# A two-layer graph network on one core: means of x taken on ScalarE and sent through DRAM, and sums and folds moved to other places

## The chip, the cores and the metric

The kernel runs on one NeuronCore of a Trainium2 chip. The metric is device time in microseconds for one launch that computes the whole output. The kernel before was run nine times; the median is 2200.85 us (2199.92 to 2202.66).

The engines are named as in the profile: PE is TensorE (matmuls; PEld its weight loads), DVE is VectorE, ACT is ScalarE, POOL is GpSimd, and SP issues most DMAs. A trailing q (SPq, PEq) means the engine's instruction queue.

## What is computed

There are 16 batches of x, 1024 nodes by 256 channels, and one adjacency matrix of 1024 by 1024. The reference, cut to what matters:

```python
# layer 0: attention whose queries come from a weighted adjacency
fea = transpose(x)                                # B, C, N
c = mean(fea, axis=1)                             # mean of x over channels: B, N
A = abs(abs(sigmoid(c[:, None, :] - c[:, :, None]) - 0.5) - 0.5) * 2
g = relu(einsum('bcn,bnm->bcm', fea, adj * A) * para)
q = heads(transpose(g));  k, v = heads(x @ kv_w)
out = softmax(q @ k.T * scale) @ v                # 4 heads of 64
x = layernorm(x + out)
# layer 1: two graph convolutions
h = relu(x @ w1_loop + adj @ (x @ w1_neigh) + b1)
h = relu(h @ w2_loop + adj @ (h @ w2_neigh) + b2)
x = layernorm(x + (x + h) * 0.5)
```

All data is float32. The channel means c enter as a row over all partitions (`c_row`) and as a column of one value per node (`c_col`); the weights of a node tile are the tanh of a scaled |c_col − c_row|, plus one, times adj.

## The kernel before

**Batches overlap.** The loop over b runs the attention of batch b in four units (two pairs of heads by two halves of the nodes). A unit's scores are eight pairs of matmuls (`s`, L516), each followed by an exponential on ACT (`pr`, L519); DVE adds the exponentials up (`acc`, L523 and L525), transposes the sum (`accB`, L527) and reduces it (`den_part`, L529). Then 32 matmuls (L536) weigh the values into `av`, which DVE transposes into `o` (L540). The softmax's denominators are finished in `add(u)`: a small matmul with the matrix `fold` (L548) sums over the 32-row groups, and DVE divides, adds to the residual `xB_a` and reduces `sums`.

In the gaps between the units stand the convolutions of earlier batches (c1, c2 and c3 are batches b−1, b−2 and b−3) and the preparation of batch b+1: `gap0` after unit 0, `gap1` after unit 1, `gap2` after unit 2. From batch 2 on, two convolutions run together as `both`, a seven-product scheme (`Joined.run`, products in the order 1, 2, 6, 7, 5, 4, 3), whose argument names the functions to be called after each product. Batch 1 has only one convolution and takes the `else` branch of gap1, with `c1.first`. Batches 2 to 14 are called the fast batches here; they all run the same instructions.

**Means before.** `prepare` (L244) transposes the channel-blocked load of x into `xT` and reduces it over the 32 channels of each block (`part`, L249, two reduces and a `join`). `means` (L262) folds `part` over partitions with one small matmul (`mean_ps`, L256), scales it, transposes a broadcast of it into `c_row` (L267), and picks `c_col` out of it with the matrix `quarter` (L269 and L272). In a fast batch it is called after product 2, in batch 1 at the head of gap1, in batch 0 between steps 6 and 7 of the queries.

**Queries.** `FastQueries` forms g with a seven-product scheme too: `step(k)` for k = 0 to 3 accumulates seven products in PSUM, two in each of three large tiles (a, b, c) and one in a bank; `end` copies product 1 to SBUF (`P1`, L482), combines them with seven adds on DVE (L483 to L489), multiplies by para (L491) and applies relu on ACT (L492). Batches 0 and 1 use the plain `Queries` (L400, end at L406 and L407).

**Normalisation.** `BlockedNorm.mean` subtracts the mean (L312). `squares` squares on ACT (L318) and reduces on DVE (L319, `sq_part`, and a join). `variance` folds that with a small matmul (`sum_ps`, L256), scales (L324) and takes the power −0.5 on POOL (L326). `scale` multiplies (L331), and `spread` transposes to `x1T` (L216) and stores to DRAM (`x1d`, L339), from which the next convolutions read.

**Keys and values.** `keys` runs two groups of eight matmuls (`k_ps`, L350), with the function `between` (the variance) called ahead of the second, and copies each group to `kT` on ACT (L352). `values` runs four groups of eight (`v_ps`, L362), each in a one-bank PSUM tile, of which there are two (`bank`, bufs=2), copied on ACT (L364). Large PSUM tiles (`big`) are three.

**Order.** The whole of `run` is under a manual schedule: each engine and each DMA queue executes in the order in which the source calls it. SBUF tiles of 128x1024 come from one pool of 23 (`row`); a tile waits until an earlier user of its buffer is through.

**Start.** x of batch 0 comes in four quarters (L117); 16 transposes on PE (L227) make its xT, then keys and values follow. `tiles` are column-blocked loads of adj (`adj_blocked`, L207) which `turn_adj` transposes on DVE (L871), in batch 1; `adj_sums` forms four sums of those tables and stores them.

Of the kernel before, what the change touches and what calls it, by code (L numbers as in the profile page):

```python
# [10 lines left out]
F32 = mybir.dt.float32  # L11
I32 = mybir.dt.int32
AF = mybir.ActivationFunctionType
# [5 lines left out]
def kernel(  # L19
# [136 lines left out]
    quarter = const.tile([P, Q], F32, name="quarter")  # L156
    nc.vector.tensor_reduce(quarter, ident.rearrange("p (i k) -> p i k", k=S), AX.X, ALU.add)
# [86 lines left out]
    def prepare(blocked, name):  # L244

        xT = channel_major(blocked, f"xT_{name}")
        part = small.tile([P, NC, NB], F32, tag="part", name=f"part_{name}", bufs=2)
        for cc in range(NC):
            nc.vector.tensor_reduce(part[:, cc, :], blocked[cc].rearrange("p (bn r) -> p bn r", r=S), AX.X, ALU.add)  # L249
        join(part)  # L250
        return xT, part

# [9 lines left out]
    def means(part, name):  # L262

        mean = small.tile([P, NB], F32, tag="mean", name=f"mean_{name}", bufs=2)
        nc.vector.tensor_scalar_mul(mean, fold_sums(part, f"mean_{name}"), 1.0 / C)
        c_row = work.tile([P, N], F32, tag="c_row", name=f"c_row_{name}")
        nc.vector.transpose(c_row.rearrange("p (bn k) -> p bn k", k=S), mean.unsqueeze(2).to_broadcast([P, NB, S]))  # L267
        own = small.tile([P, NT, Q], F32, tag="own", name=f"own_{name}", bufs=1)
        nc.vector.tensor_mul(own, mean.rearrange("p (t i) -> p t i", i=Q),  # L269
                             quarter.unsqueeze(1).to_broadcast([P, NT, Q]))  # L270
        c_col = small.tile([P, NT], F32, tag="c_col", name=f"c_col_{name}", bufs=2)
        nc.vector.tensor_reduce(c_col, own, AX.X, ALU.add)  # L272
        return c_row, c_col
# [27 lines left out]
    class BlockedNorm:  # L301
# [12 lines left out]
        def squares(self):  # L314
            self.part = small.tile([P, NC, NB], F32, tag="part", name=f"sq_part_{self.name}", bufs=2)
            for cc in range(NC):
                sq = row_tile(f"sq_{self.name}_{cc}")
                nc.scalar.activation(sq, self.xB[cc], AF.Square)  # L318
                nc.vector.tensor_reduce(self.part[:, cc, :], by_node(sq), AX.X, ALU.add)  # L319
            join(self.part)  # L320
# [89 lines left out]
    class FastQueries(Queries):  # L410
# [64 lines left out]
        def end(self):  # L475
# [10 lines left out]
            add(qT[:, 1, h0], u[:, h1], p[4])  # L486
            add(qT[:, 1, h1], u[:, h1], p[5])
# [131 lines left out]
    class GraphConv:  # L619
# [214 lines left out]
    def run():  # L834
# [5 lines left out]

        xT, c_col = prepare_first(x_first)
# [4 lines left out]
        blocked = load_blocked(1, "1")  # L846
        load_weights()
# [12 lines left out]
        tiles = {}  # L860
# [12 lines left out]
        for t in range(NT):  # L873
# [3 lines left out]
            if t == 4:  # L877
                xB = load_blocked(0, "a0")
                ready = {}
                ready["xT"], ready["part"] = prepare(blocked, "1")  # L880
            if t == 6:
                ready["mean"] = means(ready["part"], "1")
        qT = q.end()
        convs = {}
        for b in range(B):
# [9 lines left out]
            def gap0():  # L895
                blocked = load_blocked(b + 1, str(b + 1))
                c1.inner()
# [5 lines left out]
                ready["xT"], ready["part"] = prepare(blocked, str(b + 1))  # L903
# [5 lines left out]

            def next_means():  # L910
# [203 lines left out]
```

## Time and profile before

| What | Value |
|---|---|
| median of 9 runs | 2200.85 us |
| profiled execution | 2200.99 us |
| its span, first to last instruction | 2199.1 us |
| mean granted TensorE clock | 0.997 of full speed |
| first scores of batches 0, 1, 2 | 51.77, 151.50, 277.09 us |
| from one fast batch to the next | 134.7 to 135.3 us |
| DMA: x of the next batch, issue to landing | 7.2 us median |

The time that counts is the device time of a run; the profile's span leaves out some 2 us around the first and the last instruction. In the timeline a row gives the start in microseconds from the span's start, the length, engine, line, operation, tile written <- tiles read, shape, and the number of instructions merged; in brackets stands how long the engine idled before and what ended it. In the list of waits a row gives who waited for whom, the sum in microseconds, the number of times, and the longest. A matmul's length counts its way through the array; the next starts earlier. The chain that ended last (its first line gives 63% to PE, 29% to DVE) is read with care, since it names DVE's adds wherever an exponential's consumer was a bit later.

### The profile page before, as it was taken

What the parts mean: (1) busy time and instruction counts of PE and PEld (TensorE: products, weight loads), DVE (VectorE), ACT (ScalarE), POOL (GpSimd) and SP (SyncE); (2) the same over time, 40 slices, a digit from 0 to 9 for tenths busy, and PEclk for the clock granted to TensorE, in tenths of its full rate; (3) what the DMA queues carried; (4) which work ended last, traced back from release to release, by engine and by line L of the source; (5) the groups of instructions that cost most, each with busy time, mean ns of one, the idle gap of its engine ahead of it and who ended that gap; (6) DMA issues with size and microseconds to landing.
All of it is one profiled execution on the core that took longest, in us unless ns stands there. A gap on an engine that the chain in (4) does not pass through costs nothing.

```text
span 2199.1 us, 22720 instructions
## 1 busy us (share of the span) xinstructions
PE 2172.6 (99%) x8096; PEld 1031.7 (47%) x8096; DVE 1865.5 (85%) x2453; ACT 969.4 (44%) x1064; POOL 328.6 (15%) x177
## 2 busy tenths in 40 slices
PE   8998999999999999999999999999999999999998
PEld 4344444544444444444444445444454444544354
DVE  4988888898898988988889788998989889888965
ACT  4734445434354443545444454534544445434511
POOL 1010020210302103021030301203012020210021
PEclk9999999999999999999999999999999999999999
DMA  8294262633646335463453735526354262633342
GB/s 193 87 139 148 58 182 68 123 126 65 175 101 148 106 59 175 93 172 92 73 161 77 182 87 79 171 58 182 86 94 156 58 182 87 130 120 65 116 134 97
DMA packets 586359, 258.59 MB, mean 118 GB/s; under 512 B 488064, under 2 KB 552448, under 8 KB 586240
## 3 DMA queue, kind: packets, MB, share of 16 engines
q1 hardware_dynamic: 585968, 256.56, 47.9%
q8 instruction: 65, 1.06, 0.2%
q14 instruction: 54, 0.44, 0.1%
q10 hardware_dynamic: 272, 0.52, 0.1%
HBM read 210.90 MB, written 46.14 MB: 117 GB/s over the span
## 4 chain that ended last, share of the span: by engine, by line
PE 63%; DVE 29%; SPq 3%; issue 2%; DMA 1%; ACT 1%; POOL 1%; DVEq 0%; ACTq 0%
PE hu_ps L793 15%; PE s L516 13%; PE av L536 12%; DVE acc L525 7%; PE k_ps L350 4%; PE v_ps L362 4%; PE h_ps L700 2%; PE g_ps L400 2%; PE h_ps L701 2%; DVE wg L392 2%; PE hu_ps L641 2%; SPq L108 2%; PE t_ps L634 2%; DVE sq_part L319 1%; DVE wg L446 1%
## 5 line engine op out<-in xcount | busy, mean ns | idle before, releaser
L519 ACT ACTIVATE pr<-s 128x1024 f32<-128x1024 f32 x512 | 476.2, 1052 | 179.4 <-PE s L516 179.1
L525 DVE TENSOR_TENSOR acc<-acc,pr 128x1024 f32<-128x1024 f32 x384 | 493.2, 1284 | 41.4 <-DVE acc L525 0.9
L516 PE MATMUL s<-qT,kT 64*128 64x512 f32 x2048 | 457.2, 596 | 0.7 <-ACT qT L407 0.7
L536 PE MATMUL av<-pr,v 128*64 128x512 f32 x2048 | 453.6, 595 | 0.0
L516 PEld LDWEIGHTS s<-qT,kT 64*128 64x128 f32 x2048 | 190.9, 186 | 236.5 <-ACT pr L519 114.8
L536 PEld LDWEIGHTS av<-pr,v 128*64 128x64 f32 x2048 | 141.3, 137 | 300.1 <-issue 289.8
L326 POOL TENSOR_TENSOR rstd<-rstd,neg_half 128x32 f32<-128x32 f32 x16 | 87.1, 5441 | 1148.0 <-DVE rstd L324 1148.0
L386 ACT ACTIVATE wg<-c_row,c_col 128x1024 f32<-128x1024 f32 x128 | 147.1, 1149 | 87.1 <-DVE accB L527 50.6
L793 PE MATMUL hu_ps<-adj,R 128*128 128x512 f32 x360 | 158.3, 596 | 0.0
L392 DVE SCALAR_TENSOR_TENSOR wg<-wg,adj 128x1024 f32<-128x1024 f32 x128 | 149.8, 1210 | 9.8 <-ACT wg L387 9.8
L387 ACT ACTIVATE wg<-wg 128x1024 f32<-128x1024 f32 x128 | 135.4, 1058 | 4.1
L350 PE MATMUL k_ps<-xT,kvw_sb 128*128 128x512 f32 x256 | 117.2, 602 | 2.8 <-DVE U L483 2.5
L318 ACT ACTIVATE sq<-xB_a 128x1024 f32<-128x1024 f32 x32 | 33.8, 1057 | 192.3 <-DVE xB_a L312 178.7
L473 PE MATMUL g_ps<-wg,S 128*128 128x512 f32 x224 | 116.7, 603 | 0.0
L473 PE MATMUL g_ps<-T,S 128*128 128x512 f32 x224 | 114.4, 592 | 0.0
L362 PE MATMUL v_ps<-kvw_sb,xT 128*128 128x256 f32 x512 | 113.1, 379 | 0.0
L331 DVE TENSOR_TENSOR xB_a<-xB_a,rstd 128x1024 f32<-128x1024 f32 x32 | 38.8, 1254 | 84.4 <-POOL rstd L326 84.4
L473 PE MATMUL g_ps<-wg,x 128*128 128x512 f32 x224 | 109.0, 599 | 0.0
L362 PEld LDWEIGHTS v_ps<-kvw_sb,xT 128*128 128x128 f32 x512 | 97.3, 190 | 20.1 <-issue 7.7
L523 DVE TENSOR_TENSOR acc<-pr,pr 128x1024 f32<-128x1024 f32 x64 | 78.0, 1219 | 33.6 <-ACT pr L519 33.6
L793 PE MATMUL hu_ps<-adjT,t 128*128 128x512 f32 x240 | 105.7, 592 | 0.0
L793 PEld LDWEIGHTS hu_ps<-adj,R 128*128 128x128 f32 x360 | 67.3, 190 | 78.9 <-issue 74.6
(167 smaller groups left out, 2719.5 us busy)
## 6 DMA issues: line engine op xcount, KB each, us to landing
adj<-in_adj_dram SPq DMA_DIRECT2D x128, 512.0 KB, 4.5
adj<-adjT SPq DMA_DIRECT2D x120, 512.0 KB, 7.8
xB_a<-in_x_dram SPq DMA_DIRECT2D x128, 128.0 KB, 4.1
x1d<-xB_a SPq DMA_DIRECT2D x128, 128.0 KB, 3.4
x<-x1d SPq DMA_DIRECT2D x16, 1024.0 KB, 6.7
xB<-in_x_dram SPq DMA_DIRECT2D x120, 128.0 KB, 4.7
x<-in_x_dram SPq DMA_DIRECT2D x15, 1024.0 KB, 7.2
out_dram<-x SPq DMA_DIRECT2D x15, 1024.0 KB, 4.6
```

What stands on the lines that cost most here:

```text
L326: nc.gpsimd.tensor_tensor(self.rstd, self.rstd, neg_half, ALU.pow)
L350: nc.tensor.matmul(pk[:, ts(j, FB)], kvw_sb[:, cc, ts(kb, P)], xT[:, cc, ts(j, FB)], start=(cc == 0), stop=(cc == NC - 1))
L362: nc.tensor.matmul(pv[:, ts(i, C)], xT[:, cc, ts(g * per + i, P)], kvw_sb[:, cc, C:2 * C], start=(cc == 0), stop=(cc == NC - 1))
L386: nc.scalar.activation(wg, self.c_row, AF.Abs, bias=self.c_col[:, t:t + 1], scale=-1.0)
L387: nc.scalar.activation(wg, wg, AF.Tanh, scale=-0.5)
L392: nc.vector.scalar_tensor_tensor(wg, wg, 1.0, self.adj.pop(t), op0=ALU.add, op1=ALU.mult)
L473: nc.tensor.matmul(self.p[n], x_n[:, k, :], w_n, start=(k == 0), stop=(k == TJ - 1))
L516: nc.tensor.matmul(ps[:, ts(s, FB)], self.kT[rows, pair, ts(mt, P)], self.qT[rows, pair, ts(j, FB)], start=True, stop=True)
L519: nc.scalar.activation(pr, ps, AF.Exp)
L525: nc.vector.tensor_add(acc, acc, pr)
L536: nc.tensor.matmul(pav[s * HD:(s + 1) * HD, :], self.v[:, mt, pair * P + s * HD:pair * P + (s + 1) * HD], self.pr[mt][:, ts(s, FB)], start ...
L793: nc.tensor.matmul(dst, self.x[n][:, k, :], half_adj[w][:, k, :] if w else of_rows(rows, k), start=(start and k == 0), stop=(k == TJ - 1), ...
```

## The change

- The means are no longer reduced on DVE. ACT runs eight `Identity` instructions over x (128x256 each, written back in place), whose accumulator gives the node sums; POOL scales them to `c_col`. SP writes `c_col` to a line in DRAM and reads it back broadcast over 128 partitions as `c_row`. `quarter`, `prepare` and the fold of the means on PE go.
- `means` is called in gap0, right after the issue of the next batch's blocked load; for batch 0 after unit 0.
- The row sums of the squares (`sum_squares`) are split from `squares` and called inside `end`, after four of the seven adds. In the plain batch and the last batch they follow `squares` as before.
- The seven products of the queries are spread over the PSUM tiles in another way: tile b holds products 2 and 7, tile c 5 and 3.
- `keys` calls `between` later: after half of the second group.
- In batch 1, `add(1)`, `adj_sums` and the first weighing move into `c1.first`, after four of its eight node tiles.
- Before x arrives, PE runs 16 transposes of the identity into a tile that nobody reads.
- Three of the eight table loads `adj_blocked` move to the start, ahead of the weights, and their turns from batch 1 to batch 0 (step 4 of the queries).

```diff
-    quarter = const.tile([P, Q], F32, name="quarter")
-    nc.vector.tensor_reduce(quarter, ident.rearrange("p (i k) -> p i k", k=S), AX.X, ALU.add)
...
-    def prepare(blocked, name):
-
-        xT = channel_major(blocked, f"xT_{name}")
-        part = small.tile([P, NC, NB], F32, tag="part", name=f"part_{name}", bufs=2)
-        for cc in range(NC):
-            nc.vector.tensor_reduce(part[:, cc, :], blocked[cc].rearrange("p (bn r) -> p bn r", r=S), AX.X, ALU.add)
-        join(part)
-        return xT, part
...
-    def means(part, name):
-
-        mean = small.tile([P, NB], F32, tag="mean", name=f"mean_{name}", bufs=2)
-        nc.vector.tensor_scalar_mul(mean, fold_sums(part, f"mean_{name}"), 1.0 / C)
+    def means(xb, name):
+
+        c_col = small.tile([P, NT], F32, tag="c_col", name=f"c_col_{name}", bufs=2)
+        for t in range(NT):
+            nc.scalar.activation(xb[:, t, :], xb[:, t, :], AF.Identity, accum_out=c_col[:, t:t + 1])
+        nc.gpsimd.tensor_scalar_mul(c_col, c_col, 1.0 / C)
+        line = dram.tile([1, N], F32, tag="line", name=f"line_{name}")
+        nc.sync.dma_start(out=line.rearrange("o (t p) -> p (o t)", p=P), in_=c_col)
         c_row = work.tile([P, N], F32, tag="c_row", name=f"c_row_{name}")
-        nc.vector.transpose(c_row.rearrange("p (bn k) -> p bn k", k=S), mean.unsqueeze(2).to_broadcast([P, NB, S]))
-        own = small.tile([P, NT, Q], F32, tag="own", name=f"own_{name}", bufs=1)
-        nc.vector.tensor_mul(own, mean.rearrange("p (t i) -> p t i", i=Q),
-                             quarter.unsqueeze(1).to_broadcast([P, NT, Q]))
-        c_col = small.tile([P, NT], F32, tag="c_col", name=f"c_col_{name}", bufs=2)
-        nc.vector.tensor_reduce(c_col, own, AX.X, ALU.add)
+        nc.sync.dma_start(out=c_row, in_=line.to_broadcast([P, N]))
         return c_row, c_col
...
         def squares(self):
+            self.sq = [row_tile(f"sq_{self.name}_{cc}") for cc in range(NC)]
+            for cc in range(NC):
+                nc.scalar.activation(self.sq[cc], self.xB[cc], AF.Square)
+
+        def sum_squares(self):
             self.part = small.tile([P, NC, NB], F32, tag="part", name=f"sq_part_{self.name}", bufs=2)
             for cc in range(NC):
-                sq = row_tile(f"sq_{self.name}_{cc}")
-                nc.scalar.activation(sq, self.xB[cc], AF.Square)
-                nc.vector.tensor_reduce(self.part[:, cc, :], by_node(sq), AX.X, ALU.add)
+                nc.vector.tensor_reduce(self.part[:, cc, :], by_node(self.sq[cc]), AX.X, ALU.add)
             join(self.part)
...
         for kb in range(NC):
-            if kb == 1:
-                between()
             pk = big_psum(f"k_ps_{b}_{kb}")
             for j in range(NJ):
+                if kb == 1 and j == 1:
+                    between()
...
-                self.p = {1: a[:, h0], 6: a[:, h1], 7: b[:, h0], 5: b[:, h1], 2: c[:, h0], 3: c[:, h1],
+                self.p = {1: a[:, h0], 6: a[:, h1], 2: b[:, h0], 7: b[:, h1], 5: c[:, h0], 3: c[:, h1],
                           4: bank_psum(f"g_ps_{self.b}_3")}
...
-        def end(self):
+        def end(self, between):
...
             add(qT[:, 1, h0], u[:, h1], p[4])
+            between()
             add(qT[:, 1, h1], u[:, h1], p[5])
...
-        def first(self, rows01):
+        def first(self, rows01, between=None):
...
                 for mt in range(NT):
+                    if (j, mt) == (0, TJ) and between:
+                        between()
...
+        idle = bank_psum("idle")
+        for _ in range(16):
+            nc.tensor.transpose(idle[:, 0:P], ident, ident)
         xT, c_col = prepare_first(x_first)
...
         blocked = load_blocked(1, "1")
+        tiles = {mt: adj_blocked(mt) for mt in range(3)}
         load_weights()
...
             if t == 4:
                 xB = load_blocked(0, "a0")
                 ready = {}
-                ready["xT"], ready["part"] = prepare(blocked, "1")
-            if t == 6:
-                ready["mean"] = means(ready["part"], "1")
+                ready["xT"] = channel_major(blocked, "xT_1")
+                turn_adj(range(3))
...
             def gap0():
                 blocked = load_blocked(b + 1, str(b + 1))
+                q.c_row, q.c_col = means(xb, str(b + 1))
                 c1.inner()
                 att.add(0)
...
                     both.run({1: (lambda: q.left(nc.gpsimd),),
-                              2: (lambda: att.add(1), next_means),
+                              2: (lambda: att.add(1),),
...
                     q.left(nc.gpsimd)
-                    next_means()
-                    att.add(1)
                     for t in (0, TJ):
                         q.likeness(t)
                     store("01", rows01)
-                    adj_sums(rows01)
-                    weigh_first()
-                    c1.first(rows01)
+                    c1.first(rows01, lambda: (att.add(1), adj_sums(rows01), weigh_first()))
                     c1.turn_blocks()
...
+                if u == 0 and more and not between:
+                    q.c_row, q.c_col = means(xb, str(b + 1))
...
-                turn_adj(range(NT))
+                turn_adj(range(3, NT))
...
-                qT = q.end()
+                qT = q.end(norm.sum_squares)
```

More of the change, by code (lines that the diff above doesn't have):

```diff
@@ L859, in run @@
         xb = load_x(1, "1")
-        tiles = {}
         rows01 = []
@@ L902, in gap0 @@
                     both.left(nc.gpsimd)
-                ready["xT"], ready["part"] = prepare(blocked, str(b + 1))
+                ready["xT"] = channel_major(blocked, f"xT_{b + 1}")
             def weigh_first():
@@ L908, in weigh_first @@
                 q.right(0)
-            def next_means():
-                q.c_row, q.c_col = means(ready["part"], str(b + 1))
             def gap1():
@@ L962, in run @@
                     else:
-                        q.c_row, q.c_col = ready["mean"]
                         for t in range(3):
@@ L975, in run @@
                     q.likeness(t)
-                for mt in range(4):
-                    tiles[mt] = adj_blocked(mt)
+                tiles[3] = adj_blocked(3)
                 q.times_adj(3)
@@ L992, in run @@
                 norm.squares()
+                norm.sum_squares()
                 q.step(5)
@@ L1023, in run @@
                 both.fetch(1, 4)
-                both.run({1: (lambda: att.add(3),), 2: (norm.mean, norm.squares), 7: (norm.variance,),
+                both.run({1: (lambda: att.add(3),), 2: (norm.mean, norm.squares, norm.sum_squares), 7: (norm.variance,),
                           5: (norm.scale, norm.spread)})
@@ L1064 @@
             xb = load_x(b, "z")
-            xT, part = prepare(load_blocked(b, "z"), "z")
+            xT = channel_major(load_blocked(b, "z"), "xT_z")
             q = Queries("z", xb)
-            q.c_row, q.c_col = means(part, "z")
+            q.c_row, q.c_col = means(xb, "z")
             kT, v = keys("z", xT), values("z", xT)
```

## The prediction

> **What bounds the kernel now.** I read the page's first lines, then TensorE's waits, then the timeline at the few places where TensorE stands still.
>
> ```profile
> span 2199.1 us, 22720 instructions
> PE 2172.6 (99%) x8096; PEld 1031.7 (47%) x8096; DVE 1865.5 (85%) x2453; ACT 969.4 (44%) x1064; POOL 328.6 (15%) x177
> PE den_ps L548 <- DVE o L540: 5.6, 1, 5.6
> PE xT_ps L227 <- DMA x<-in_x_dram: 4.9, 2, 4.7
> PE k_ps L350 <- DVE U L483: 2.5, 12, 0.5
> ```
>
> TensorE is busy 99% of the span and waits for others in three places worth a name: 5.6 us once, 4.7 us at the start, 2.5 us over twelve batches. So the change pays only through those and through TensorE work it drops. DVE time saved elsewhere is worth nothing by itself, and any wait put on TensorE costs its full length, up to 14 times.
>
> The 5.6 us lie in batch 1, between two attention units:
>
> ```profile
> 183.59 0.41 PE L256 MATMUL mean_ps<-part,fold 128*128 128x32 f32 x2
> 188.79 0.71 DVE L540 STREAM_TRANSPOSE o<-av 128x512 f32<-128x512 f32 x1
> 189.55 0.64 PE L548 MATMUL den_ps<-den_part,fold 128*128 128x32 f32 x2 [5.55 <-DVE o L540]
> 190.00 3.30 PE L641 MATMUL h_ps<-x1T,w1l_sb 128*128 128x512 f32 x4
> 208.68 7.14 PE L516 MATMUL s<-qT,kT 64*128 64x512 f32 x32
> 223.62 0.41 PE L548 MATMUL den_ps<-den_part,fold 128*128 128x32 f32 x2 [0.78 <-DVE den_part L529]
> ...
> 189.50:192.70 3.20, 3.15 (x6) 1.60 (x6) 3.05 (x10) 1.49 (x2) 0.00 (x0) 0.50 0.00 0
> ```
>
> The last row is of the view by windows (stretch, length, busy time of each engine, granted clock, DMA). The clock fell to 0.50 during the idle time, at 185.9, and stays there 3.2 us after it: the four L641 take 3.30 us, against 1.88 us at 200.01.
>
> The end of a fast batch (batch 4 into 5) is the other place:
>
> ```profile
> 665.57 0.57 ACT L482 COPY P<-g_ps 128x512 f32<-128x512 f32 x1
> 667.06 0.68 DVE L483 TENSOR_TENSOR U<-P,g_ps 128x512 f32<-128x512 f32 x1
> 667.79 3.70 PE L350 MATMUL k_ps<-xT,kvw_sb 128*128 128x512 f32 x8 [0.16 <-DVE U L483]
> 671.62 2.36 DVE L491 TENSOR_TENSOR qT<-qT,para_sb 128x1024 f32<-128x1024 f32 x2
> 672.88 2.19 ACT L492 ACTIVATE qT<-qT 128x1024 f32<-128x1024 f32 x2 [6.75 <-DVE qT L491]
> 674.98 1.91 ACT L352 COPY kT<-k_ps 128x1024 f32<-128x1024 f32 x2
> 674.98 7.07 PE L362 MATMUL v_ps<-kvw_sb,xT 128*128 128x256 f32 x32
> 676.91 0.58 ACT L364 COPY v<-v_ps 128x512 f32<-128x512 f32 x1
> ```
>
> The reader is to see that ScalarE runs here without a pause, relu, two kT copies, first v copy, and that the v copy ends at 677.49. The v_ps groups of eight matmuls are 1.73 us apart (the later copies at 678.64, 680.36 and 682.09 show it), so the third starts at 678.44, in the bank which that copy frees (there are two). The slack is 0.95 us.
>
> **The change, part by part** (against the profiled execution, 2200.99 us with a span of 2199.1; the median is 2200.85).
>
> *Means, TensorE.* The fold leaves the stream: in batch 5 it starts at 722.89 and the next matmul at 723.12, so 0.23 us, in 13 fast batches −3.0 us. Batch 0's is followed 0.14 us later by the next matmul: −0.1. Batch 1's lies in the stall below.
>
> *Means, DVE.* Two reduces of 1.15, a join, a scale, a transpose of 1.25 and two small ones leave each batch, some 4.3 us. In the fast batches I cost this at nothing: DVE waits for TensorE at the second L705 (0.97 us at 763.47), after all that is removed, and its chain from there to the queries is the same as before.
>
> *Means, ScalarE.* Eight instructions of 128x256 stand between unit 0's exponentials and the t1 copy, where ScalarE idles 9.35 us. They need x of the next batch: issued at 687.62, landing 7.2 us later by the page's median, so 694.8; the t1 copy is at 699.94. An Identity with accumulation is not in the trace. Nearest is L731, an Identity of the same shape, eight in 4.04 us; a copy of twice the size takes 0.58, a floor of about 3 us for eight; 0.59 each without overlap gives 4.7 us. The slack of 5.1 us shrinks to 4.2 (below: x comes 1.6 later, the copy 0.7). By 4.04 it fits on the median; landing times differ between batches, so I charge +1.0 in all; bounds 0 and +6.5 (0.5 in 13 batches).
>
> *Means, queues.* SP gets two DMAs behind the next batch's blocked load, and the second waits for the first. Bounds: 3.4 us (1024 small packets, the x1d row) and 4.5 us (512 KB, the adj row). Behind them stand load_x and the fetch of tables 2 and 3, issued from 701.4 on and landing 7.8 later, by 713; product 6 needs them at 723.1. Pushed by 1.6+3.4 and the 4.5 of c_row they come near 722.5: hidden, by little. On POOL an operation of 128x8 (under 0.2 us as the 128x32 memsets of 0.12) stands before R; R is used after 714 and starts at 698.5: hidden. If these covers failed, product 6 would wait.
>
> *Fold of the squares and the reordered ends.* Now U waits for L319's two reduces and the join; afterwards it follows the P copy (ends 666.14). TensorE is through with g_ps at 667.47 (666.61 plus two at 0.43) and k_ps starts at 667.79; without the wait 0.24 earlier, 14 times: −3.4 us. But the reduces (667.06 − 664.56 = 2.5 us) now stand in the middle of the adds. DVE ends L312 at 664.51 and then idles until the P copy at 666.14: 1.6 us that the reduces had filled. So four adds to 668.7, reduces to 671.2, three adds to 673.2, the two L491 to 675.6, against 673.98. The relu, both kT copies and the first v copy all come 1.6 later: v copy at 678.5, done 679.1. TensorE, 0.24 earlier, wants its bank at 678.2. New stall: 1.62 + 0.24 − 0.95 = 0.91 us, 14 times: +12.7; bounds 0 and that. The scores after it start 0.7 later. The moved fold (L256) needs the join at 671.2 and comes at 672.7: no wait. Behind the late L491 stand rstd, POOL's power, the scale, the x1d stores and so x: the 1.6 us used above.
>
> *Batch 1.* The unit's den fold moves behind twelve matmuls of 0.43, from 183.6 to 188.9. DVE, spared 2.45 us of reduces (174.70 to 177.15), has den_part at 186.4: no stall, no cold clock; the convolution of 17.7 us ends at 201.3 instead of 208.68. That is not kept: DVE is the longer chain there. From rden at 189.2: adds 2.8, adj_sums 9.3, weights and T 4.95, h1B 1.2, acc 9.2, den_part 2.5, so 219.2, while TensorE's av ends at 215.5. The fold that came at 223.62 comes at 219.25: −4.4. The new idle time of 3.8 us is enough for the clock to fall again (before, it fell 2 us into one); cold matmuls cost 1.6 us by the same rows (3.30 against 1.88, and the fold). I take −2.8; bounds −0.5 and −7.2.
>
> *The Trainium skill* (TensorE: Matmul & The Clock Gate, Part 1) says the clock gate judges free-running windows of about 3.4 us; the low clock of 6.8 us above is two of them. By its rule that only a whole idle window re-throttles, the new idle time would be at the edge, and batch 1 would give −4.4.
>
> *Start.* Sixteen transposes from 1.5 us on.
>
> ```profile
> 4.70 1.09 PE L227 MATMUL xT_ps<-ident,x 128*128 128x128 f32 x4 [4.70 <-DMA x<-in_x_dram]
> 5.97 2.69 PE L227 MATMUL xT_ps<-ident,x 128*128 128x128 f32 x12 [0.18 <-DMA x<-in_x_dram]
> 8.49 3.60 PE L350 MATMUL k_ps<-xT,kvw_sb 128*128 128x512 f32 x8
> 11.99 1.06 PE L239 MATMUL mean_ps<-ident,c_col 128*128 128x128 f32 x8
> ```
>
> Twelve cold transposes take 2.69 us, eight warm ones 1.06. The third and fourth quarter of x, 0.26 MB each at the 397 GB/s of the stretch from 5 to 10 us, follow the second (5.97) 0.66 apart, so 7.3; warm, the last four transposes take 0.5 more, and k_ps starts near 8.0, 0.5 earlier. Cold, the sixteen (0.22 each) last to 5.1, past x by 0.4. I take −0.5; bounds −0.5 and +0.4.
>
> *The same page* (Part 4) says transposes don't engage the full clock. Here nothing but transposes ran before 8.49, and k_ps runs at 0.45 a matmul at once, as at 667.79: the row decides. By the rule the start would bring 0.
>
> *Table turns.* Twelve loads move ahead of the weights; at 1.27 us each (10.17 for 8 at 29.89) they are issued by 40 and landed by 44.5; six turns of 0.6 fit before L406 at 49.40, where DVE sat idle 9.1 us. Six turns fewer later: DVE there ends 0.35 before it is needed, nothing waits. 0; if the loads came 5 us later still, each us would count.
>
> Sum: −3.0 − 0.1 + 1.0 − 3.4 + 12.7 − 2.8 − 0.5 = +3.9, so **2204.9 us**.
>
> **Rivals.** *No tail stall*: if the late relu doesn't reach the v copies (a faster ScalarE chain, a third bank), the +12.7 and the late x (+1.0) go: 2191. For it: TensorE shows no wait for ScalarE there today. Against: the order on ScalarE is fixed and its rows leave 0.95 us. *Means too dear* (slower): each accumulating instruction takes 0.59 without overlap; from 4.2 us for eight on, the t1 copy, and unit 1's exponentials 0.2 us behind it, come late. 0.5 us in 13 batches on top: 2211. *The stall in batch 1 doesn't come back*: its 7.2 us kept whole, 4.4 more: 2200.5.
>
> **How the numbers follow.** Forecast 0.50 (own range 2200 to 2209), no stall 0.20, dear means 0.20, batch 1 whole 0.10. The range from 2190 to 2212 takes all in. This measurement can't tell less than 0.2% (4.4 us) from no change, so faster is under 2196.4 and slower over 2205.2. The forecast lies on the upper edge: half of its cases slower, the rest within. Faster: 0.20; within: 0.25 + 0.10 = 0.35; slower: 0.25 + 0.20 = 0.45.
>
> **What would show it.** Right: a TensorE wait of near 1 us at v_ps for the copy L364, fourteen times; L491 ending 8 us after g_ps, not 6.5; no den_ps wait at 184 but one of 3 to 4 us a unit later. Wrong: v_ps without a wait; an accumulating instruction over 0.6 us; SP's queue late for product 6; a fold of the squares that TensorE waits for.

## The result, and the profile after

The changed kernel takes 2214.1 us (median of 10 runs, 2208.5 to 2217.8) against 2201.2 us of the kernel before in the same session (30 runs, 2199.8 to 2204.2): a ratio of 1.0055, 95% interval [1.0047, 1.0063]. It is slower by about 12 us, more than this kernel's measurement scatters, and its own scatter of 9 us is twice that of the kernel before. The profiled execution took 2212.47 us, with this head on its page:

```profile
span 2210.6 us, 22846 instructions
...
PE 2175.6 (98%) x8082; PEld 1031.1 (47%) x8082; DVE 1805.3 (82%) x2347; ACT 1015.9 (46%) x1304; POOL 333.0 (15%) x192
```

DVE lost 60 us of work and PE has 14 instructions fewer, yet the span grew by 11.5 us. The list of waits (who waited for whom: sum, times, longest) says where; PE, DVE and SP's queue each have a list:

```profile
PE v_ps L353 <- ACT v L355: 11.7, 13, 1.0
PE den_ps L540 <- DVE den_part L521: 8.1, 6, 3.8
...
PE hu_ps L787 <- DMA adj<-adjT: 1.4, 4, 0.6
...
DVE xT L214 <- DMA xB<-in_x_dram: 27.2, 9, 5.0
...
SPq L260 <- DMA line<-c_col: 134.8, 15, 11.4
```

In the kernel before, DVE's waits for the same load sum to 1.8 us:

```profile
DVE xT L216 <- DMA xB<-in_x_dram: 1.8, 4, 0.8
```

The first line of the changed kernel's list is the forecast tail stall, 0.90 us in each of 13 batches. The second has the forecast 3.8 us of batch 1 and five waits that were not forecast. The last two lead to their cause: DVE waits for the last DMA of the blocked x, and SP stands 9 us in each batch between the write of the line of means and its reading. That is also in the DMA issues (size, median us from issue to landing):

```profile
adj<-adjT SPq DMA_DIRECT2D x120, 512.0 KB, 10.2
...
x<-x1d SPq DMA_DIRECT2D x16, 1024.0 KB, 9.0
...
c_row<-line SPq DMA_DIRECT2D x15, 512.0 KB, 6.1
...
line<-c_col SPq DMA_DIRECT2D x15, 4.0 KB, 9.5
```

The smallest transfer of the batch, 4 KB, takes the longest but one. In the kernel before, the fetch of the tables and the x1 load were quicker:

```profile
adj<-adjT SPq DMA_DIRECT2D x120, 512.0 KB, 7.8
...
x<-x1d SPq DMA_DIRECT2D x16, 1024.0 KB, 6.7
```

For an account I measured the time between the first exponentials of neighbouring attention units. "Start" runs from the last unit of a batch to the first of the next (14 of them, batches 2 to 15); "third unit" from the second unit to the third (batches 2 to 14, around the joined convolution). From before to after: the first exponential of all −0.35 us; batch 1 (first to last unit) 72.45 to 68.89, so −3.56; starts 53.18 to 53.92 each (medians), +9.6 in all; third units 550.8 to 556.3 in all, +5.5; the other units are the same to 0.01 us; 0.4 remain behind the last start. The +5.5 hide two things: the floor of a third unit fell from 42.20 to 41.97 (13 × −0.23 = −3.0), while what lies over the floor grew from 2.2 to 10.7 us (+8.5), unevenly: 0 in three batches, 3.8 in batch 13. There one sees how it comes about. SP's queue and DVE, from the timeline of batch 13:

```profile
1785.80 0.67 SPq L108 DMA_DIRECT2D xB<-in_x_dram  x1
1786.57 0.51 SPq L258 DMA_DIRECT2D line<-c_col  x1
1796.93 0.35 SPq L260 DMA_DIRECT2D c_row<-line  x1
1797.34 0.43 SPq L619 DMA_DIRECT2D x<-x1d  x1
```

```profile
1788.00 1.23 DVE L214 STREAM_TRANSPOSE xT<-xB 128x1024 f32<-128x1024 f32 x1
1794.20 1.25 DVE L214 STREAM_TRANSPOSE xT<-xB 128x1024 f32<-128x1024 f32 x1 [4.97 <-DMA xB<-in_x_dram]
```

The last blocked load is issued just ahead of the line. The one before it landed at 1788.40; this one at 1794.08, 5.7 us later, where the others follow one another by some 0.9 us. DVE's accumulation of the second unit is behind that transpose, so den_part comes at 41.5 us after the batch's first exponential; TensorE can use it at 39.6. That is 2.0 of the 3.8 us. The rest is TensorE's clock, which fell to 0.50 soon after the wait (by windows: stretch, length, busy time of PE, PEld, DVE, ACT, POOL, granted clock, DMA share, GB/s):

```profile
1807.06:1808.87 1.81, 0.01 (x2) 0.00 (x1) 1.78 (x3) 0.00 (x0) 0.00 (x0) 1.00 1.01 405
1808.87:1809.81 0.94, 0.94 (x4) 0.70 (x5) 0.94 (x2) 0.00 (x0) 0.92 (x1) 1.00 1.02 405
1809.81:1813.22 3.41, 3.41 (x5) 1.33 (x5) 3.30 (x8) 0.00 (x0) 1.57 (x2) 0.50 1.03 410
```

### The profile page after: what moved, and what is told of

The parts are those of the page before. It is cut to its first block, busy times and chain, and to the rows that moved or that the text cites. A ratio compares the mean times of both kernels' runs of the same rounds, so it can differ in the third digit from the quotient of the medians.

```text
span 2210.6 us, 22846 instructions
## 1 busy us (share of the span) xinstructions
PE 2175.6 (98%) x8082; PEld 1031.1 (47%) x8082; DVE 1805.3 (82%) x2347; ACT 1015.9 (46%) x1304; POOL 333.0 (15%) x192
## 4 chain that ended last, share of the span: by engine, by line
PE 48%; DVE 29%; DMA 8%; issue 7%; ACT 3%; SPq 3%; POOL 2%; DVEq 0%; ACTq 0%; POOLq 0%
PE hu_ps L787 13%; PE s L508 11%; PE av L528 10%; DVE acc L517 6%; PE h_ps L694 2%; PE g_ps L391 2%; PE h_ps L695 2%; DMA adj<-adjT 2%; DVE wg L383 2%; DMA xB<-in_x_dram 2%; PE hu_ps L633 2%; POOL rstd L317 2%; DMA line<-c_col 2%; PE v_ps L353 2%; SPq L108 2%
## 5 line engine op out<-in xcount | busy, mean ns | idle before, releaser
L353 PE MATMUL v_ps<-kvw_sb,xT 128*128 128x256 f32 x512 | 116.9, 382 | 11.8 <-ACT v L355 11.7
```

What stands on the lines that cost most here:

```text
L353: nc.tensor.matmul(pv[:, ts(i, C)], xT[:, cc, ts(g * per + i, P)], kvw_sb[:, cc, C:2 * C], start=(cc == 0), stop=(cc == NC - 1))
```

## The experiments

All times are medians; "to before" is against the kernel before in the same session. The columns are the units as above (a start is the median of 14); "over" is the sum of the third units over their floor.

| kernel | us | to before | start | third: floor, over | batch 1 |
|---|---|---|---|---|---|
| before | 2201.2 | | 53.18 | 42.20, 2.2 | 72.45 |
| changed | 2214.1 | +12.9 | 53.92 | 41.97, 10.7 | 68.89 |
| e1_sums_early | 2199.0 | −2.3 | 53.19 | 41.97, 3.6 | 68.53 |
| e2_means_before | 2215.1 | +13.8 | 53.94 | 42.20, 8.1 | 71.04 |
| e3_both_undone | 2199.9 | −1.4 | 53.19 | 42.20, 0.6 | 71.05 |
| e4_line_last | 2209.3 | +8.0 | 53.94 | 41.97, 5.5 | 68.77 |
| e5_line_last_early | 2195.2 | −6.3 | 53.20 | 41.97, 1.9 | 68.08 |
| e6_line128_early | 2193.8 | −7.8 | 53.20 | 41.97, 0.0 | 69.17 |
| e7_line128 | 2203.1 | +1.6 | 53.94 | 41.97, 0.0 | 68.28 |
| e8_line128_after_mult | 2213.6 | +12.1 | 53.23 | 41.86, 0.0 | 69.16 |
| e9_split_sums | 2188.2 | −13.3 | 52.81 | 41.97, 0.0 | 69.16 |
| e10_split_b1_later | 2197.1 | −4.5 | 52.81 | 41.97, 0.0 | 77.75 |
| e11_start_alone (one run) | 2200.7 | −0.8 | 53.19 | 42.20, 1.3 | 73.05 |
| e12_means_alone | 2202.1 | +0.6 | 53.19 | 41.97, 12.4 | 69.82 |

**The squares put back** (e1_sums_early):

```diff
-                q.step(2, lambda: (norm.mean(), norm.squares()))
+                q.step(2, lambda: (norm.mean(), norm.squares(), norm.sum_squares()))
-                qT = q.end(norm.sum_squares)
+                qT = q.end(lambda: None)
```

> The changed kernel with the two reduces of the squares back directly behind the squares (so ahead of the adds that put Q together), everything else as changed. Theory (two costs that add up: the late values of V, and the slow write of the line of means): the waits of v_ps for the copy of V go (11.7 us in 13 waits), the step at each batch's start falls from about +0.73 us to about -0.2 us, and the time falls by 11 to 13 us, to about 2202 us. Rival 1 (the reduces in front of the adds bring back the wait of k_ps for U): a step of about 0 at each batch's start, 2204 us. Rival 2 (the wait of v_ps only stands in for another that is as late, such as scores for Q): the step stays above +0.5 us and the time above 2211 us.

2199.0 us, ratio 0.9997 [0.9985, 1.0008], 15 us under the changed kernel, more than the 11 to 13 expected. The v_ps waits are gone and the starts lost 0.73 us each. They came back only to 53.19, where the kernel before had them: the wait of k_ps for U returned (2.5 us in 13 waits). So rival 1 named the mechanism and the size of the starts rightly; neither expectation had the 7 us that the third units gave back (10.7 to 3.6 over their floor). Its runs scatter from 2195.0 to 2212.5 us.

**The means put back** (e2_means_before; `prepare`, `quarter` and `means` as before, called where they were before, in batch 1 ahead of the likeness):

```diff
+            def next_means():
+                q.c_row, q.c_col = means(ready["part"], str(b + 1))
...
-                              2: (lambda: att.add(1),),
+                              2: (lambda: att.add(1), next_means),
```

> The changed kernel with the means as in the kernel before (reduces on VectorE, fold on TensorE, no line through DRAM, no accumulating Identity), everything else as changed. Theory: the steps at the third unit of each batch, which sum to +5.5 us over batches 2 to 14 in the changed kernel and scatter from -0.8 to +3.2 us, go to 0 within 0.3 us each; the time falls by 5 to 6 us, to about 2208.5 us. Rival (the eight accumulating instructions and the line are hidden, and the scatter comes from the moved folds and the reordered products): the steps scatter as before and the time stays within 2 us of 2214 us.

2215.1 us, 1.0060 [1.0047, 1.0073]: no gain, a miss. The third units still lie 8.1 us over their floor, without any line in DRAM. The rival's time is right. What follows is read from the traces: all waits in the third units here are for DVE, whose own waits for the blocked x sum to 7.6 us, against 0.4 in e3 below. The cause is in the distances to a batch's first exponential: DVE's den_part comes at 38.9 us in an undisturbed batch of the kernel before, against the 39.6 at which TensorE wants it; with the squares among the adds, the first store of x1 goes out 1.4 us ahead of that exponential instead of 2.2, all of SP's later loads move with it, and the 0.7 us of slack are gone. With the new means that slack is 3.2 us (den_part at 36.4), so the same delay is free there, as e7 below shows. Why single waits for the blocked x reach 1.7 us, where the stores are only 0.9 us later, no run shows.

**Both put back** (e3_both_undone: the two edits above together):

> The changed kernel with both put back: the means as before, and the reduces of the squares directly behind the squares. What is left of the change is the start, batch 1, the early table turns, the new order of the seven products in the accumulators, and the fold of the squares later in K. Theory: the two costs add, so the time falls by 16 to 19 us, to about 2196 us, below the kernel before by the start (0.35), batch 1 (3.6) and the wait of k_ps (up to 3.4). Rival (the two costs overlap, a late V hides a late line): the fall is that of the larger one alone, to about 2202 us.

2199.9 us, 0.9995 [0.9986, 1.0004], a miss: neither 2196 nor simply the larger cost alone. The third units are at their old floor, 0.6 us over it in all. What is left of the change brings 1.4 us here, as much as batch 1 gains by it.

**The line behind the fetch** (e4_line_last; `row_of` holds the two DMAs that stood in `means`):

```diff
                 if both:
                     c2.load_x()
                     both.fetch(2, 3)
                     both.left(nc.gpsimd)
+                q.c_row = row_of(q.c_col, str(b + 1))
```

> The changed kernel with the two DMAs of the line of means (write to DRAM, read back as a row) issued after the load of the blocked batch's x1 and the fetch of tables 2 and 3 instead of ahead of them; the eight accumulating instructions stay. Theory (SP is held by the write, 9.5 us, and the write's 4-byte pieces delay the last load of the blocked x that is issued just ahead of it): the load of x1 and the fetches are issued 9 us earlier, the last blocked load lands about 1 us behind the one before, the steps at the third unit fall to about -0.2 us each, and the time falls by 6 to 8.5 us, to about 2206 us. Rival 1 (only the accumulating instructions on ScalarE matter): no change, 2214 us. Rival 2 (the row of means then comes too late for the likeness): a new wait of ScalarE for the row, and the time rises by 5 us or more.

2209.3 us, 1.0042 [1.0030, 1.0054], a part of the expected gain. DVE's waits for the blocked x fell from 27.2 to 3.4 us, so the write did delay that load. But beside the fetch the write took 14.5 us (median), and now TensorE waited for the fetched table in four batches (2.7 us) and for a copy of ScalarE in two (1.4 us).

**The same line in larger pieces** (e7_line128). VectorE turns the column in 32x32 blocks, so that each piece of the line is 32 numbers long:

```diff
-        c_col = small.tile([P, NT], F32, tag="c_col", name=f"c_col_{name}", bufs=2)
+        c_pad = small.tile([P, S], F32, tag="c_pad", name=f"c_pad_{name}", bufs=2)
+        nc.gpsimd.memset(c_pad, 0.0)
+        c_col = c_pad[:, 0:NT]
...
-        nc.sync.dma_start(out=line.rearrange("o (t p) -> p (o t)", p=P), in_=c_col)
+        c_turn = small.tile([P, S], F32, tag="c_turn", name=f"c_turn_{name}", bufs=2)
+        nc.vector.transpose(c_turn, c_pad)
+        by_block = line.rearrange("o (t a k) -> (o t) a k", a=Q, k=S)
+        for a in range(Q):
+            nc.sync.dma_start(out=by_block[:, a, :], in_=c_turn[a * S:a * S + NT, :])
```

> The changed kernel, the squares' reduces where the change has them, with the line of means written in 128-byte pieces: VectorE turns the column of means in blocks of 32x32 and four DMAs of 1 KB each write 32 pieces of 128 bytes, at the place where the change issues one DMA with 1024 pieces of 4 bytes. Theory (the 4-byte pieces make the write slow, 9.5 us, and keep the last load of the blocked x, which is in flight beside it, from landing): each write lands within 4 us, the last blocked x lands 1 us behind the one before in every batch, VectorE's waits for it fall from 27.2 us to under 6 us, the sum of the third units' excess over 41.97 us falls from 10.7 us to under 3 us, and the time falls by 7 to 9 us, to about 2206 us. The 14 starts of a batch stay at 53.92 us. Rival 1 (the write is slow because it is a DRAM write behind others, whatever its pieces): the write takes 8 us or more and the time stays at 2214 us. Rival 2 (the late squares alone delay the blocked x): the waits for the blocked x stay above 20 us and the time stays at 2214 us.

2203.1 us, 1.0008 [0.9999, 1.0017], 11.0 us below the changed kernel, in a band of 1.7 us (2202.7 to 2204.4). From its waits:

```profile
PE v_ps L359 <- ACT v L361: 12.6, 13, 1.3
PE den_ps L546 <- DVE den_part L527: 3.8, 1, 3.8
...
DVE xT L214 <- DMA xB<-in_x_dram: 0.3, 1, 0.3
...
SPq L266 <- DMA line<-c_turn: 25.0, 25, 2.2
```

SP's wait fell from 134.8 to 25.0 us, DVE's from 27.2 to 0.3, and all 13 third units are at 41.97 us. The tail stall stays, as it must. Same data, same place, same number of bytes: the write's form alone was worth 11 us. The trace gives no landing times for these four DMAs, so "within 4 us" is not shown directly; SP stood 25.0 us for them in 15 batches, 1.7 us each on average. The gain is larger than expected, in part since the median of the changed kernel lies 1.6 us above its profiled execution.

**Line and squares together** (e5_line_last_early: e4's and e1's edits; e6_line128_early: e7's and e1's).

> The changed kernel with the squares' reduces directly behind the squares and the two DMAs of the line issued after the load of x1 and the fetch of tables 2 and 3. Theory: the 14 starts take 53.19 us, as with the reduces alone put back, and no blocked x is delayed by the write; the third units keep some excess where the fetched table comes late beside the write. Time about 2195 us, 3 to 5 us below that with the reduces alone put back and the line in its place (2199.0 us). Rival (the write in flight beside the fetch costs as much as it did beside the blocked x): 2199 us.

> The changed kernel with the squares' reduces directly behind the squares and the line of means in 128-byte pieces, in the place of the change. Theory: starts at 53.19 us, third units at 41.97 us with an excess below 2 us in all, so about 3 us less than with the reduces alone put back, and little scatter from run to run: about 2195 us, below the kernel before by 6 us. Rival (four issues on SP hold the x1 load and the fetch as long as the one slow write did): 2199 us.

2195.2 us, 0.9970 [0.9960, 0.9981], and 2193.8 us, 0.9964 [0.9951, 0.9978]; both as the theories had it. The runs now form a table: with the squares ahead of the adds 2199.0 (4-byte pieces) and 2193.8 (128 bytes), with them among the adds 2214.1 and 2203.1. The late squares cost 9.3 us beside a quick line, nearly all in the starts, and 15.1 beside the slow one; the slow line costs 5.2 or 11.0. The two costs share some 6 us. A likely reason, not tested by itself: the stores of x1 that the squares delay push the blocked loads, and the slow line holds the last of these.

**The squares later still** (e8_line128_after_mult, on e7; in `values` the function is called ahead of the third group):

```diff
             add(qT[:, 1, h0], u[:, h1], p[4])
-            between()
             add(qT[:, 1, h1], u[:, h1], p[5])
...
                 nc.scalar.activation(qT[:, cb, :], qT[:, cb, :], AF.Relu, scale=QSCALE)
+            between()
             return qT
...
-                kT = keys(b + 1, xT, norm.variance)
-                norm.scale()
-                norm.spread()
-                v = values(b + 1, xT)
+                kT = keys(b + 1, xT)
+                v = values(b + 1, xT, between=lambda: (norm.variance(), norm.scale(), norm.spread()))
```

> The changed kernel with the line of means in 128-byte pieces and the squares' reduces moved on, behind the two products with the per-channel parameters that end Q, and the variance, the scaling and its transposes and stores moved from K into V. Theory (what delays V is that the products that end Q, and so ScalarE's relu and copies, stand behind the reduces; the reduces themselves cost nothing while VectorE has spare time there): no wait of v_ps, no wait of k_ps, starts of a batch at 52.9 to 53.0 us; stores of x1 no later than in the changed kernel; time about 2190 us, which beats both kernels. Rival 1 (the stores come later and the blocked x with them): third units with an excess over 41.97 us of 5 us or more, 2196 us or above. Rival 2 (TensorE's fold of the squares then waits inside V): a wait of about 1 us in each batch, 2204 us.

2213.6 us, 1.0055 [1.0042, 1.0069]; no expectation named this loss. The starts fell to 53.23 us (with 0.3 us each for a bank that V shares with the folded squares), but the unit after each start grew from 18.00 to 19.55 us, 20 us over 13 batches:

```profile
PE s L516 <- ACT t L637: 4.6, 9, 0.9
PE v_ps L361 <- DVE rstd L321: 4.0, 14, 0.3
...
ACT x L257 <- DMA x<-in_x_dram: 104.1, 13, 8.8
```

The stores of x1 go out 3.3 us later against the batch's first exponential, the load of x behind them on SP too, and the eight Identity wait for it on ScalarE 104.1 us (63.1 with the squares among the adds). The t1 copy stands behind them. This is the prediction's rival of dear means, brought about not by the price of the instructions but by a late load.

**One reduce ahead, one among the adds** (e9_split_sums, on e7):

```diff
-                q.step(2, lambda: (norm.mean(), norm.squares()))
+                q.step(2, lambda: (norm.mean(), norm.squares(), norm.sum_squares((0,))))
-                qT = q.end(norm.sum_squares)
+                qT = q.end(lambda: norm.sum_squares((1,)))
```

> The changed kernel with the line of means in 128-byte pieces and the two reduces of the squares split: the first directly behind its square, where VectorE otherwise idles until ScalarE's copy of product 1, the second with the join between the adds, where the change has both. Theory (two reduces among the adds make the relus 1.6 us late against a slack of 0.95 us; one of 1.22 us moved back leaves about 0.4 us, which the slack covers): no wait of v_ps and no wait of k_ps, starts of a batch at 52.9 to 53.1 us against 53.92 us with both among the adds and 53.19 us with both ahead, third units at 41.97 us; time 2190 to 2193 us. Rival (any work of VectorE among the adds is paid one for one): starts at 53.5 us, 2198 us.

2188.2 us (2188.2 to 2189.7), 0.9940 [0.9927, 0.9954]: faster than both kernels, and a little under the range expected. Its waits:

```profile
PE den_ps L548 <- DVE den_part L529: 3.8, 1, 3.8
...
PE v_ps L361 <- ACT v L363: 0.2, 1, 0.2
...
DVE U L482 <- ACT P L481: 5.4, 14, 0.4
```

One reduce of 1.22 us fills DVE's idle time before the copy of product 1 down to 0.4 us, the other stays within the slack; neither k_ps nor v_ps waits, and a start takes 52.81 us.

**Batch 1** (e10_split_b1_later, on e9): the call of `between` in `first` at `(1, TJ)` instead of `(0, TJ)`.

> As the split of the reduces, and in batch 1 the fold of the second unit, the table sums and the first weights are issued later still inside its convolution: before the fifth table block of the second half instead of the first half. Theory A (TensorE only came 3.8 us too early to that fold, and the idle time then also halves its clock for about 3 us): the wait of den_ps for den_part in batch 1 goes from 3.8 us to below 0.5 us, the clock in batch 1 stays at 1.00, and the time falls by 4 to 5 us against the split alone. Theory B (VectorE, 0.98 busy there, is the bound of batch 1): the wait goes but comes back at the next unit or at batch 2's start, and the time changes by less than 1 us.

2197.1 us, 0.9980 [0.9970, 0.9989], 8.8 us slower than e9: against both theories, and nearest to B. The folds of TensorE and DVE's wait for the first of them:

```profile
197.06 0.30 PE L548 MATMUL den_ps<-den_part,fold 128*128 128x32 f32 x2
...
227.37 0.64 PE L548 MATMUL den_ps<-den_part,fold 128*128 128x32 f32 x2 [9.94 <-DVE den_part L529]
```

```profile
184.81 1.22 DVE L529 TENSOR_REDUCE den_part<-accB 128x32 f32<-128x1024 f32 x1
...
197.40 0.52 DVE L552 RECIPROCAL rden<-den_ps 64x16 f32<-64x16 f32 x2 [10.75 <-PE den_ps L548]
...
226.10 1.22 DVE L529 TENSOR_REDUCE den_part<-accB 128x32 f32<-128x1024 f32 x1
```

DVE sets the pace from 187 on, and all its work there waits for the unit's own fold. In e9 it waited 2.2 us for it, here 10.75, and the next unit's wait on TensorE grew from 3.8 to 9.9. During TensorE's wait the clock fell to 0.50 and stayed there from 220.20 to 233.85. So the fold must not come so late that DVE stands waiting for it. Nor is earlier always better: in e12 below, with the new means and the fold where the kernel before has it, TensorE waits 3.11 us for den_part ahead of the convolution, and batch 1 takes 69.82 us against 68.89 in the changed kernel (e12 lacks the early table turns as well).

**Start and means by themselves** (e11_start_alone: the kernel before with the 16 transposes; e12_means_alone: the kernel before with the changed `means`).

> The kernel before with the 16 transposes into an unused bank ahead of its first transposes, and nothing else. Theory (the changed kernel's start gains 0.35 us at the first exponential, of which the fold on TensorE that is gone explains 0.23 us): the first exponential at 53.2 to 53.35 us, against 53.34 us before. Rival (the busy TensorE makes the first products faster): 53.0 us or less.

> The kernel before with the new means alone: eight accumulating Identity on ScalarE, the column of means through DRAM in 4-byte pieces, no reduces of x on VectorE and no fold of the means on TensorE; the squares, batch 1, the start and the order of the products as before. Theory: third units have their floor at 41.97 us instead of 42.20 us and an excess of 2 to 6 us in all from late blocked loads, batch 1 falls by about 2 us since VectorE binds there and has less to do, starts stay at 53.18 us; about 2197 us with a wide scatter from run to run. Rival (the new means are what makes the changed kernel slow, whatever the squares do): 2206 us or more.

e11's first exponential came at 53.06 us, 0.28 earlier and between the two expectations; with the old means e2 and e3 had it at 53.34 and 53.28 with the same transposes, so the start gives 0 to 0.3 us as the first loads land. e12 took 2202.1 us, 1.0002 [0.9993, 1.0011], from 2197.9 to 2208.6, above the 2197 expected. The line took 9.9 us there, and in the profiled execution (span 2206.6, the slowest but one of its eleven runs) DVE waited 26.7 us for blocked loads and the third units lay 12.4 us over their floor. So the slow line does harm with the squares in their old place, too.

## Why the prediction was wrong, by its steps

It said 2204.9 us, 2190 to 2212; 2214.1 came. The step that failed is "Means, queues": 0, "hidden, by little", with 3.4 us for the write of the line, taken from the row of the x1 stores. Measured: 9.5 us for the write (and 6.1 for the reading back, where 4.5 was put), and 11.0 us of run time (e7 against the changed kernel). Without it, e7 lies at 2203.1, 1.8 us from the forecast. That closeness is in part luck: in e7 the starts cost 11.1 us and not 9.3, and the third units gave 5.2 and not 3.0, since the 2.2 us over the floor that the kernel before has went too. Two things were wrong in that step. The x1 row was no bound from above: its pieces are 128 bytes, those of the line 4, and 1024 of them are another matter than 1024 of the larger. And I looked for the harm only behind the write, at product 6; most of it was ahead of it, at a load that was already in flight. In the list of waits TensorE waits 1.4 us in all for the fetched tables.

- *Means, TensorE*, −3.0: right, the floor of the third unit fell by 0.23 us in 13 batches.
- *Means, DVE*, 0: right for the queries. But the new means leave den_part 2.5 us earlier (36.4 for 38.9), slack that would have covered the late loads of e2, and batch 1 gained from it (below).
- *Means, ScalarE*, +1.0: 0; the first units stayed at 18.00 us. An accumulating Identity takes 0.40 us on the engine, its reading of the accumulator 0.19 beside the next:

```profile
L255 ACT ACTIVATE x<-x x120: 398/401/490, 60.2 to 1921.3; 128x256 f32<-128x256 f32 x120
L255 ACT ACTIVATION_READ_ACCUMULATOR x<-x x120: 185/187/264, 60.5 to 1921.6; 128x1 f32 x120
```

  (The group of that line in the changed kernel; ns, shortest, median, longest.) Eight take 3.2 us, not 4.04. So the rival "dear means" fell; that its 2211 us lies nearer to the result than the forecast is luck.
- *Fold of the squares*, −3.4 and +12.7: the mechanism is shown, by the timeline of batch 4 into 5 and by e1 and e9. The rows of the changed kernel:

```profile
664.22 0.57 ACT L473 COPY P<-g_ps 128x512 f32<-128x512 f32 x1
...
664.82 0.69 DVE L474 TENSOR_TENSOR U<-P,g_ps 128x512 f32<-128x512 f32 x1 [1.66 <-ACT P L473]
...
667.41 2.34 DVE L310 TENSOR_REDUCE sq_part<-sq 128x32 f32<-128x1024 f32 x2
...
671.93 2.36 DVE L483 TENSOR_TENSOR qT<-qT,para_sb 128x1024 f32<-128x1024 f32 x2
673.18 2.19 ACT L484 ACTIVATE qT<-qT 128x1024 f32<-128x1024 f32 x2 [8.39 <-DVE qT L483]
...
677.08 1.09 ACT L355 COPY v<-v_ps 128x512 f32<-128x512 f32 x2
677.73 3.72 PE L353 MATMUL v_ps<-kvw_sb,xT 128*128 128x256 f32 x16 [0.89 <-ACT v L355]
```

  DVE idles 1.66 us until P, the reduces stand behind four adds, the relu, the copies of K and the first copy of V follow late, and TensorE waits 0.89 us where 0.91 was forecast. Net +9.3 forecast, +9.6 measured. e9 shows the other half: where neither wait is left, a start takes 0.37 us less than before, so taking the reduces from ahead of the adds was worth up to 0.37 and not 0.24.
- *Batch 1*, −2.8: −3.56. The new idle time is 3.8 us, as forecast, and the clock fell again:

```profile
218.00:219.00 1.00, 0.21 (x2) 0.21 (x2) 1.00 (x2) 0.00 (x0) 0.00 (x0) 1.00 0.00 0
219.00:220.00 1.00, 1.00 (x4) 0.56 (x5) 1.00 (x2) 0.00 (x0) 0.00 (x0) 0.60 0.00 0
220.00:221.00 1.00, 1.00 (x6) 0.38 (x4) 1.00 (x2) 0.00 (x0) 0.00 (x0) 0.50 0.00 0
...
222.00:223.00 1.00, 1.00 (x6) 0.35 (x4) 0.93 (x5) 0.38 (x2) 0.00 (x0) 0.69 1.01 393
```

  TensorE stands idle from 214.98 to 218.79; the clock falls at 219.2 and is low for 3.4 us, in which the 32 score matmuls take 8.83 us instead of 7.14. The Trainium skill (TensorE: Matmul & The Clock Gate, Part 1) has the low clock follow a whole idle window of about 3.4 us, which put 3.8 us at the edge. The traces do not fit that: at the fall TensorE had worked again for 0.4 us; in batch 1 of the kernel before the clock fell after 1.88 us of idle time (184.00 to 185.88); and in batch 13 of the changed kernel an idle time of 1.80 us was enough, while one of 1.95 us in e12 was not. Nor is the price fixed: in e6, e8 and e9, with the same 3.8 us of idle time, the clock was low for 6.8 us, and batch 1 took 69.2 us. The origin was half wrong: with the old means the new order brings 1.4 us (e3), the new means alone 2.6 (e12).
- *Start*, −0.5: the first exponential came 0.35 us earlier, with the −0.1 of batch 0's fold in it. In e2 and e3, with the same transposes and the old means, it came 0.00 and 0.06 us earlier, but x landed 0.2 to 0.3 us later there than in the kernel before; so the start's own part is not settled between 0 and 0.3. The rule on transposes that the prediction quotes does not hold here: in e7 only transposes had run when those of x began, and the first four of x took 0.60 us, against 1.09 in the kernel before.
- *Table turns*, 0: no wait appeared there.

The rival "no tail stall" fell with 11.7 us of v_ps waits; "batch 1 whole" fell with den_ps. The forecast's warning, "SP's queue late for product 6", stood next to the right place.

## What to carry to other kernels

This write was priced by its pieces, not its bytes: before a column over the partitions is written out number by number, turn it so that each piece is a row, and look what loads are in flight beside it. Work that filled an engine's idle time before a dependent chain is not free once it stands inside the chain; move only as much as the slack takes (one reduce of two: 5.6 us better than both ahead, 15 us better than both inside). And where one engine paces a stretch, the small operation of another engine that releases it must not come later than the first can use it (8.8 us in e10).

## What was unexpected of the hardware

A write of 4 KB in 1024 pieces took 8.5 to 11.9 us, 10.9 us in batch 0 with next to no other traffic, and 14.5 us (median) beside the fetch of two tables. For most of that time no traffic is on record; batch 13 of the changed kernel, by windows, with the line and the last blocked load outstanding until 1796.87 and 1794.08:

```profile
1788.00:1789.00 1.00, 1.00 (x8) 0.38 (x4) 1.00 (x2) 1.00 (x3) 0.92 (x2) 1.00 0.70 24
...
1791.00:1794.00 3.00, 3.00 (x16) 1.06 (x16) 0.00 (x0) 1.75 (x2) 0.00 (x0) 1.00 0.00 0
1794.00:1796.00 2.00, 2.00 (x12) 0.61 (x10) 1.80 (x2) 0.00 (x0) 0.00 (x0) 1.00 0.00 0
```

So the bytes had gone by about 1789 and the reports came 5 and 8 us later. The trace records the completion of these transfers in 16 parts: fifteen of the load's came by 1788.88 and one at 1794.08, those of the line from 1792.27 to 1796.87. Why the small pieces delay the report, and part of that of a load issued ahead of them with it, the trace does not show. That the form of the write decides it, e7 does; and that it is the size of the pieces and not their number, the x1 stores suggest, which take 3.5 us with 1024 pieces of 128 bytes. Which batches are hit differs from kernel to kernel with this write (one execution of each was profiled), and the scatter of the times goes with it: 9 us in the changed kernel, 1.5 to 1.7 us in e6, e7 and e9.
